# Edge counts and masked attention of a graph network in one written order, with one-hot rows made six chunks ahead

## The chip, the cores and the metric

The kernel runs on one core of a Trainium2 chip. The metric is the device time of one execution in microseconds (us). Three runs of the kernel before gave a median of 616.33 us (615.88 to 616.94).

## The reference

Four layers of a graph network run one after the other on 512 nodes with 512 features. The graph has 16,896 directed edges, sorted by their destination, each of one of two types. The change touches the first layer, an attention over all node pairs that is masked by the edges; cut to its core:

```python
q = (x @ Wq + bq).reshape(N, H, HEAD)          # N = 512, H = 8, HEAD = 64; k and v likewise
scores = jnp.einsum('nhd,mhd->nhm', q, k) / np.sqrt(HEAD)
adj = jnp.zeros((N, N)).at[edge_index[0], edge_index[1]].set(1.0)
scores = jnp.where(adj[:, None, :] == 0, -1e9, scores)
attn = softmax(scores, axis=1)                 # over the heads
attn_out = jnp.einsum('nhm,mhd->nhd', attn, v).reshape(N, D_OUT) @ Wo + bo
h1 = layer_norm(x + attn_out)
return layer_norm(h1 + relu(h1 @ W1 + b1) @ W2 + b2)
```

The softmax runs over the eight heads of one pair of nodes, so that one 128-row tile of pairs needs nothing of another tile. The layers behind it add up neighbours (two layers of a network with batch norm, one graph convolution, two layers with a weight matrix for each edge type). The weight matrices of the last two layers are mixtures of 30 matrices of 512 x 512 each:

```python
w = jnp.einsum('rb,bio->rio', att, basis)      # basis: 30 x 512 x 512, att: 2 x 30
```

This mixture depends on no node, so that it can be worked out at any time before the last layers.

## The kernel before

**Counts.** All layers need the edges as matrices of 512 x 512: how many edges of each type lead from a node to another. The kernel counts them on TensorE. The edges lie in 132 chunks of 128. For each chunk `chunk` (L406) makes two one-hot rows for each edge: `hd`, the destination inside the tile, weighted by the type (VectorE, L416), and `hs`, the source among 512 nodes (ScalarE's Sign, L420, for the chunks of PSUM bank 0; VectorE, L422, for those of bank 1). One matmul (L425) of the two adds the chunk's counts into `cnt`. As the edges are sorted, each of the four destination tiles takes a contiguous span of about 35 chunks; a chunk on a border belongs to two tiles, is made once and is kept. The rows have six buffers a tag. `counted` (L428) decodes a tile's two banks into `Bc` with three copies on ScalarE and three operations on VectorE, and updates the mask `apart`.

**Attention.** It has eight blocks: two halves of 256 nodes (`part`) times four tiles of 128 neighbours (`mt`). `attention` (L477) is a generator of seven steps: two half scores (mask matmuls L484 and key times query L489 into `psc`, which has one buffer, and a copy on ScalarE, L491), the maximum over the heads on VectorE (L494 to L496), the subtraction there and the exp on ScalarE (L498, L499), the sum over the heads as eight matmuls with the identity (by the helper `product`, L244) and a reciprocal on VectorE (L504), the weighting (L506), and the products with v (L514) into `ao`. Blocks 0 to 2 of the first half run beside the counts of tiles 1 to 3, one step for every five chunks; the five other blocks follow two at a time. The products for q and k run beside the counts of tile 0, the four for v beside those of tile 1, one for every eight chunks.

**Basis.** `basis_step` (L181) works off the mixture of basis matrices in 64 steps of four matmuls each (L191), 32 for each of the last two layers. Each takes a 960 KB load on SP's queue, kept four ahead. After each fourth step ScalarE copies the result and stores it to DRAM (`summed`), from where `wrel_load` (L199) fetches it on POOL's queue. The steps are strewn over the program: 4, 6, 6 and 6 in the counts of the four tiles, 10 in the attention, two in the loop with Wo (`basis_step(t % 2)`, L634), four in that with W1 (L658), and the others later.

**Order.** A scheduler sets each engine's order of instructions from their dependencies and its estimate of their times; the order of the program is only where it starts. `tc.keep_in_program_order(...)` holds the instructions that are given to it in the program's order. Before, it holds the basis steps and a few others; the counts and the attention are left to the scheduler. Waits between engines are semaphores, and an engine runs its own instructions in order.

Of the kernel before, what the change touches and what calls it, by code (L numbers as in the profile page):

```python
# [30 lines left out]
LESS = 2.0 ** -12  # L31
MARGIN = 2
SIGNED = (14, 24, 24, 24)
AHEAD = 4
EPS = 1e-5
SLOPE = 0.01
# [30 lines left out]
def gnn_kernel(ctx: ExitStack, tc: tile.TileContext, out: bass.AP, a: dict):  # L67
# [27 lines left out]


    ep = edges.enter_context(tc.tile_pool(name="edges", bufs=1))
    op = edges.enter_context(tc.tile_pool(name="onehot", bufs=6))
    raw = ExitStack()
    rp = raw.enter_context(tc.tile_pool(name="raw", bufs=1))  # L100

# [140 lines left out]
    def product(p, pairs):  # L242
        for i, (lhsT, rhs) in enumerate(pairs):
            nc.tensor.matmul(p, lhsT=lhsT, rhs=rhs, start=(i == 0), stop=(i == len(pairs) - 1))  # L244

    def ts(i):
        return slice(i * P, (i + 1) * P)

    def flip(src, s, dst=None):

        p = ps()
        for k in range(T):
            nc.tensor.transpose(p[:, ts(k)], src[:, s, ts(k)], ident)  # L253
        p = p.rearrange("q (k n) -> q k n", k=T)
        if dst is None:
            return p
        nc.scalar.copy(dst[:, :, ts(s)], p)
# [125 lines left out]
    def project_v():  # L383
        w = weights.take()
        v = made["v"] = big("E")
        bv = rows.take()
        for t in range(T):
            p = ps()
            product(p, [(made["hT"][:, k, ts(t)], w[:, k, :]) for k in range(T)])
            nc.vector.tensor_add(v[:, t, :], p, bv)  # L390
            yield


# [9 lines left out]
    assert all(len(cs) <= 31 for pair in in_bank for cs in pair)  # L403
    kept = {}

    def chunk(c, t, cnt):  # L406

        b = bank_of[c]
        if c in kept:
            hd, hs, first = kept.pop(c)  # L410
        else:
            first = tiles_of[c][0]
            both = len(tiles_of[c]) == 2
            w = P * len(tiles_of[c])
            hd = op.tile([P, 2 * P], F16, name="hd", tag="hd2" if both else "hd", bufs=4 if both else 6)
            nc.vector.tensor_scalar(hd[:, :w], iot[:, P * first:P * first + w], key[:, 0, c:c + 1],  # L416
                                    key[:, 2, c:c + 1], op0=ALU.is_equal, op1=ALU.mult)
            hs = op.tile([P, N], F16, name="hs", tag="hs2" if both else "hs", bufs=4 if both else 6)
            if b == 0:
                nc.scalar.activation(hs, iot, AF.Sign, bias=key[:, 3, c:c + 1])  # L420
            else:
                nc.vector.tensor_scalar(hs, iot, key[:, 1, c:c + 1], None, op0=ALU.is_equal)  # L422
            if both:
                kept[c] = hd, hs, first
        nc.tensor.matmul(cnt[b], lhsT=hd[:, ts(t - first)], rhs=hs,  # L425
                         start=(c == in_bank[t][b][0]), stop=(c == in_bank[t][b][-1]))

    def counted(t, cnt):  # L428

        left = ep.tile([P, N + 1], F32, name="left")  # L430
        nc.scalar.copy(left[:, 1:], cnt[0])
        nc.scalar.activation(left[:, 0:1], cnt[0][:, N - 1:N], AF.Copy, scale=-1.0)
        nc.scalar.copy(Bc[1][:, t, :], cnt[1])
        nc.vector.tensor_sub(Bc[0][:, t, :], cnt[0], left[:, :N])
        for held in (cnt[1], Bc[0][:, t, :]):
            nc.vector.scalar_tensor_tensor(apart[:, t, :], held, 0.0, apart[:, t, :], op0=ALU.is_equal, op1=ALU.mult)

    def typed(t, rest):

# [34 lines left out]
                for i in range(2):  # L474
                    yield 4 * q + 2 * b + i, 2 * q + i, b

    def attention(part, mt):  # L477
        ns = slice(part * NH, (part + 1) * NH)
        qT, kT = made["q"], made["k"]
        sc = pool[0].tile([P, H, NH], F32, name="sc")  # L480
        for q in range(2):
            p = psum[0].tile([P, 2, 2, NH], F32, tag="sc", name="psc", bufs=1)
            for b in range(2):
                nc.tensor.matmul(p[:, b], lhsT=far_off, rhs=apart[:, mt, None, ns].to_broadcast([P, 2, NH]),  # L484
                                 start=True, stop=False)
            for i in range(2):
                for b in range(2):
                    bs = slice(HD * b, HD * b + HD)
                    nc.tensor.matmul(p[:, b, i, :], lhsT=kT[bs, 2 * q + i, ts(mt)], rhs=qT[bs, 2 * q + i, ns],  # L489
                                     start=False, stop=(i == 1))  # L490
            nc.scalar.copy(sc[:, 4 * q:4 * q + 4, :], p.rearrange("p b i n -> p (b i) n"))  # L491
            yield
        half = pool[0].tile([P, H // 2, NH], F32, name="half", bufs=1)
        nc.vector.tensor_max(half, sc[:, 0:4, :], sc[:, 4:8, :])  # L494
        nc.vector.tensor_max(half[:, 0:2, :], half[:, 0:2, :], half[:, 2:4, :])
        nc.vector.tensor_max(half[:, 0, :], half[:, 0, :], half[:, 1, :])  # L496
        yield
        nc.vector.tensor_sub(sc, sc, half[:, 0:1, :].to_broadcast([P, H, NH]))  # L498
        nc.scalar.activation(sc, sc, AF.Exp, scale=HD ** -0.5)  # L499
        yield  # L500
        p = bank("ps")[:, :NH]
        product(p, [(ident, sc[:, j, :]) for j in range(H)])
        rec = pool[0].tile([P, NH], F32, name="rec", bufs=2)
        nc.vector.reciprocal(rec, p)  # L504
        yield
        nc.vector.tensor_mul(sc, sc, rec[:, None, :].to_broadcast([P, H, NH]))  # L506
        yield
        if mt == 0:

            ao[part] = [bank(("ao", "cnt")[part]) for _ in range(2)]  # L510
            for j in range(2):
                nc.tensor.matmul(ao[part][j], lhsT=zero[:, :P], rhs=zero, start=True, stop=False)
        for s, hp, b in heads():
            nc.tensor.matmul(  # L514
                ao[part][hp // 2][HD * b:HD * b + HD, hp % 2 * NH:hp % 2 * NH + NH],
                lhsT=made["v"][:, mt, (2 * hp + b) * HD:(2 * hp + b + 1) * HD], rhs=sc[:, s, :],
                start=False, stop=False)
        if mt == T - 1:
            for j in range(2):
                nc.tensor.matmul(ao[part][j], lhsT=zero[:, :P], rhs=zero, start=False, stop=True)  # L520
                nc.scalar.copy(aoT[:, 2 * j:2 * j + 2, ns], ao[part][j].rearrange("p (i n) -> p i n", i=2))
        yield

    def chain(*gens):
        for g in gens:
# [4 lines left out]
            next(gen, None)  # L530

    proj = chain(project_T(BQ, "C", "q"), project_T(BK, "D", "k"))
    proj_v = project_v()
    for t in range(T):
        cnt = [bank("cnt") for _ in range(2)]
        side = attention(0, t - 1) if t else None
        n = 0
        if t == 1:
            advance(proj_v)
            advance(side)  # L540
        for c in range(*span[t]):
            chunk(c, t, cnt)
            n += 1
            if t == 0 and n == 12:
                select()
                raw.close()
                pool.append(edges.enter_context(tc.tile_pool(name="attn", bufs=3)))
            if t == 0 and n % 4 == 0:
                advance(proj)
            if t == 1 and n % 8 == 0:  # L550
                advance(proj_v)
            if t and n % 5 == 3:
                advance(side)
            if n % 6 == 5 and (t or n > 16):
                basis_step()
        if t:
            for _ in side:
                pass
        counted(t, cnt)
        if t == 0:  # L560
            for _ in proj:
                pass
        if t == 1:
            for _ in proj_v:
                pass
            aoT = big("B")

    under = []
    for block in ((0, 3), (1, 0), (1, 1), (1, 2), (1, 3), None, None):
        if len(under) == 2 or not block:  # L570
            for _ in under.pop(0):
                pass
            basis_step(1)
        if under:
            advance(under[-1], 2)
        if block:
            under.append(attention(*block))
            advance(under[-1], 2)
            basis_step(1)
    edges.close()  # L580
    psum.append(ctx.enter_context(tc.tile_pool(name="psum2", bufs=1, space=bass.MemoryType.PSUM)))
    turn[0] = ["pr", "pr", "pg"]
# [42 lines left out]
    for t in range(T):  # L625
        p = ps()
        product(p, [(aoT[:, k, ts(t)], w[:, k, :]) for k in range(T)])
        v = h1[:, t, :]
        nc.vector.tensor_add(v, p, bo)
        nc.vector.tensor_add(v, v, h[:, t, :])  # L630
        norm_affine(v, g1, be1)
        if t:
            flip(h1, t - 1, h1T)
            basis_step(t % 2)  # L634
    rest = [late.tile([P, T, N], F32, tag="wrel", name="rest", bufs=2) for _ in range(2)]
    for t in range(T):
        typed(t, rest)
# [10 lines left out]
    for half in range(2):  # L648
        ns = slice(half * NH, (half + 1) * NH)
        for i in range(2):  # L650
            for m in range(T):
# [3 lines left out]
                nc.scalar.activation(ff[i][:, m, ns], p[:, :NH], AF.Relu, bias=cols[:, at:at + 1])  # L655
                if half == 0 and i == 0 and m == 2:
                    flip(h1, T - 1, h1T)
            basis_step(1)  # L658
    w = [weights.take(), weights.take()]
    b2, g2, be2 = (rows.take() for _ in range(3))  # L660
    y, hT = big("A"), big("D")
# [289 lines left out]
```

## Time and profile before

| what | value |
|---|---|
| median of three runs | 616.33 us (615.88 to 616.94) |
| the profiled execution | 616.2 us |
| its span | 614.4 us |
| mean granted TensorE clock | 0.967 |
| TensorE (PE) busy | 554.8 us, 90% of the span, 2226 instructions |
| TensorE weight loads (PEld) | 277.1 us, 45% |
| VectorE (DVE) | 275.4 us, 45%, 590 instructions |
| ScalarE (ACT) | 199.1 us, 32%, 319 instructions |
| GpSimd (POOL) | 32.9 us, 5%, 70 instructions |
| DMA | 94.06 MB, 153 GB/s over the span |

The profiled execution is one, and its span starts and ends with the first and last instruction; its time includes 1.8 us around that. A row of a timeline has the start in us from the span's beginning, the duration in us, the engine, the line and the operation, output and inputs with partitions x elements and type, how many instructions it joins, and in brackets how long the engine idled before it and whose result ended that idle time. Three of the costliest groups, with the busy time, the mean ns of one and the idle time before them:

```profile
L420 ACT ACTIVATE hs<-iot,key 128x512 f16<-128x512 f16 x80 | 52.9, 713 | 17.0 <-PE cnt L425 16.4
L425 PE MATMUL cnt<-hs,hd 128*128 128x512 f16 x144 | 41.3, 391 | 6.3 <-DVE hs L422 5.6
L491 ACT COPY sc<-psc 128x1024 f32<-128x1024 f32 x16 | 16.1, 1006 | 27.9 <-PE psc L489 27.9
```

### The profile page before, as it was taken

The page shows a single profiled execution, that of the slowest core. Times are in us where ns is not written, and L with a number is a line of the kernel's source. Part 1 is how long each engine was busy: PE and PEld are TensorE (multiplying, and loading weights), DVE is VectorE, ACT ScalarE, POOL GpSimd, SP SyncE. Part 2 cuts the span into 40 slices and gives each one's busy share as a digit, 9 for nine tenths or more (in the row PEclk, how much of TensorE's full clock was granted, in tenths as well). Part 3 has the DMA queues.
Part 4 walks back from the last instruction along what each step waited for, and adds up shares of the span by engine and source line. Part 5 has one row for each costly group of instructions (what it writes and reads, how often), then busy time and mean ns, then how long its engine had stood idle before and what let it go on. Part 6 is the DMA issues. An engine that isn't in the chain of part 4 may idle for free.

```text
span 614.4 us, 5939 instructions
## 1 busy us (share of the span) xinstructions
PE 554.8 (90%) x2226; PEld 277.1 (45%) x2226; DVE 275.4 (45%) x590; ACT 199.1 (32%) x319; POOL 32.9 (5%) x70
## 2 busy tenths in 40 slices
PE   2999999797878867899999999999869899999997
PEld 1433343333344433367544453353324556545653
DVE  4732665665464852489076632422511841103110
ACT  3534566465333410222233221522332260104100
POOL 4000000000000000010202100000000200000000
PEclk9999999797998988899999999999969999999999
DMA  8998779899783672468987856786699000003000
GB/s 290 217 243 177 202 173 253 190 203 199 165 191 79 146 178 64 97 179 198 313 199 200 217 152 156 177 206 197 180 225 221 8 18 2 0 1 138 1 34 34
DMA packets 42345, 94.06 MB, mean 153 GB/s; under 512 B 1949, under 2 KB 2345, under 8 KB 41801
## 3 DMA queue, kind: packets, MB, share of 16 engines
q1 hardware_dynamic: 34296, 67.32, 48.3%
q0 software_dynamic: 5136, 21.07, 10.6%
q10 hardware_dynamic: 2880, 5.24, 2.6%
q8 instruction: 21, 0.34, 0.2%
q14 instruction: 12, 0.09, 0.1%
HBM read 88.38 MB, written 5.24 MB: 152 GB/s over the span
## 4 chain that ended last, share of the span: by engine, by line
PE 49%; issue 35%; DMA 7%; DVE 3%; ACT 1%; POOL 1%; POOLq 0%; ACTq 0%
PE pr L244 11%; PE acc L868 9%; PE pg L244 8%; DMA row<-in_rows 5%; PE acc L833 5%; PE ao L244 4%; PE bas L191 4%; PE ps L244 3%; DMA basis<-in_basis 2%; PE cnt L425 2%; PE acc L704 1%; PE acc L244 1%; PE pr L253 1%; POOL w L138 0%; ACT hs L420 0%
## 5 line engine op out<-in xcount | busy, mean ns | idle before, releaser
L191 PE MATMUL bas<-basis,wide 120*32 120x512 f32 x512 | 72.7, 629 | 7.0 <-DMA basis<-in_basis 6.9
L420 ACT ACTIVATE hs<-iot,key 128x512 f16<-128x512 f16 x80 | 52.9, 713 | 17.0 <-PE cnt L425 16.4
L416 DVE TENSOR_SCALAR hd<-iot,key 128x128 f16<-128x128 f16 (+1 forms) x132 | 36.5, 314 | 35.6 <-PE cnt L425 35.4
L244 PE MATMUL ps<-sc,ident 128*128 128x256 f32 x128 | 37.8, 451 | 14.0 <-ACT sc L499 13.6
L425 PE MATMUL cnt<-hs,hd 128*128 128x512 f16 x144 | 41.3, 391 | 6.3 <-DVE hs L422 5.6
L244 PEld LDWEIGHTS ps<-sc,ident 128*128 128x128 f32 x128 | 28.0, 227 | 25.3 <-ACT sc L499 16.6
L425 PEld LDWEIGHTS <-hd 128*128 128x128 f16 x144 | 12.6, 99 | 43.7 <-issue 19.1
L244 PE MATMUL pr<-w,bigB 128*128 128x512 f32 x64 | 30.3, 620 | 0.0
L868 PE MATMUL acc<-wrel,bigC 128*128 128x512 f32 x64 | 29.7, 593 | 0.0
L191 PEld LDWEIGHTS bas<-basis,wide 120*32 120x32 f32 x512 | 10.8, 110 | 35.0 <-issue 25.0
L491 ACT COPY sc<-psc 128x1024 f32<-128x1024 f32 x16 | 16.1, 1006 | 27.9 <-PE psc L489 27.9
L504 DVE RECIPROCAL rec<-ps 128x256 f32<-128x256 f32 x8 | 14.0, 1755 | 23.0 <-PE ps L244 23.0
L269 ACT ACTIVATE sd<-mv,eps 128x1 f32<-128x1 f32 x32 | 9.2, 293 | 44.8 <-DVE mv L267 43.7
L499 ACT ACTIVATE sc<-sc 128x2048 f32<-128x2048 f32 x8 | 15.3, 1910 | 21.1 <-DVE sc L498 21.1
L494 DVE TENSOR_TENSOR half<-sc 128x1024 f32<-128x1024 f32 x8 | 9.8, 1225 | 27.5 <-ACT sc L491 27.5
L244 PE MATMUL pr<-bigE,w 128*128 128x512 f32 x48 | 21.2, 592 | 0.0
L244 PE MATMUL pr<-bigD,w 128*128 128x256 f32 x88 | 20.3, 381 | 0.0
L244 PEld LDWEIGHTS pr<-w,bigB 128*128 128x128 f32 x64 | 12.6, 203 | 17.1 <-issue 15.9
L489 PE MATMUL psc<-bigC,bigD 64*128 64x256 f32 x128 | 19.5, 404 | 0.0
L244 PE MATMUL ao<-bigB,w 128*128 128x512 f32 x40 | 19.1, 616 | 0.0
L506 DVE TENSOR_TENSOR sc<-sc,rec 128x2048 f32<-128x2048 f32 x8 | 18.3, 2287 | 0.2
L422 DVE TENSOR_SCALAR hs<-iot,key 128x512 f16<-128x512 f16 x52 | 18.0, 349 | 0.6 <-DVEq L360 0.6
(293 smaller groups left out, 894.3 us busy)
## 6 DMA issues: line engine op xcount, KB each, us to landing
basis<-in_basis SPq DMA_DIRECT2D x64, 960.0 KB, 9.3
w<-in_W POOLq DMA_DIRECT2D x4, 1024.0 KB, 5.9
summed<-sums ACTq DMA_DIRECT2D x16, 256.0 KB, 8.1
wrel<-summed POOLq DMA_DIRECT2D x4, 1024.0 KB, 5.7
row<-in_rows POOLq DMA_DIRECT2D x12, 256.0 KB, 7.8
w<-in_conv_W1T POOLq DMA_DIRECT2D x2, 1024.0 KB, 7.1
w<-in_conv_W2T POOLq DMA_DIRECT2D x2, 1024.0 KB, 6.6
w<-in_root POOLq DMA_DIRECT2D x2, 1024.0 KB, 6.5
```

Source lines behind the costliest of these rows:

```text
L191: tc.keep_in_program_order(nc.tensor.matmul(sums[0][32 * j:32 * j + 32, :], lhsT=wide[l][:KB, 24 - 8 * g:56 - 8 * g], rhs=t[:, j, :], star ...
L244: nc.tensor.matmul(p, lhsT=lhsT, rhs=rhs, start=(i == 0), stop=(i == len(pairs) - 1))
L416: nc.vector.tensor_scalar(hd[:, :w], iot[:, P * first:P * first + w], key[:, 0, c:c + 1], key[:, 2, c:c + 1], op0=ALU.is_equal, op1=ALU.mult)
L420: nc.scalar.activation(hs, iot, AF.Sign, bias=key[:, 3, c:c + 1])
L422: nc.vector.tensor_scalar(hs, iot, key[:, 1, c:c + 1], None, op0=ALU.is_equal)
L425: nc.tensor.matmul(cnt[b], lhsT=hd[:, ts(t - first)], rhs=hs, start=(c == in_bank[t][b][0]), stop=(c == in_bank[t][b][-1]))
L489: nc.tensor.matmul(p[:, b, i, :], lhsT=kT[bs, 2 * q + i, ts(mt)], rhs=qT[bs, 2 * q + i, ns], start=False, stop=(i == 1))
L491: nc.scalar.copy(sc[:, 4 * q:4 * q + 4, :], p.rearrange("p b i n -> p (b i) n"))
L499: nc.scalar.activation(sc, sc, AF.Exp, scale=HD ** -0.5)
L506: nc.vector.tensor_mul(sc, sc, rec[:, None, :].to_broadcast([P, H, NH]))
L833: nc.tensor.matmul(self.out[t], lhsT=self.hT[:, k, ts(t)], rhs=self.root[:, k, :], start=(k == 0), stop=False)
L868: nc.tensor.matmul(self.out[t], lhsT=self.uT[r][:, k, ts(t)], rhs=wrel[r][:, k, :], start=False, stop=(r == 1 and k == T - 1))
```

## The change

The counts of tiles 1 to 3 and all of the attention stand in one written order on TensorE, VectorE and ScalarE: the helper `on` puts each of their instructions under `keep_in_program_order`. Tile 0 with q and k stays with the scheduler.

`chunk` is split in two, `rows_of` and `count`. In tiles 1 to 3 the rows of a chunk are emitted six chunks (`BEHIND`) ahead of their matmul, and the pool has seven buffers for them in place of six. The steps of the attention, now methods of a class `Block` with the same instructions, stand at set places of a tile's count: `weigh` of the block before behind count 1, `shift` behind count 8, `values` of the block before behind count 15, `sums` behind count 22, basis steps behind counts 5, 18 and 30. At the tile's end come `counted`, two basis steps and the scores of the next block. Of the four products for v the first stands before tile 1, two in it (behind counts 2 and 12) and one in tile 2 (behind count 12). The blocks of the second part follow in a loop: values of block j-2, scores of j+1, shift of j, a basis step, weigh of j-1, sums of j.

The basis steps move: 26 instead of 32 stand before the stage with Wo (3 in tile 0, 15 with tiles 1 to 3, 8 in the attention), 3 instead of 2 in the loop with Wo, 6 instead of 4 in that with W1; the other places ask for as many as before, and three steps more are left for the last place in the program, which works off what remains.

```diff
-    op = edges.enter_context(tc.tile_pool(name="onehot", bufs=6))
+    op = edges.enter_context(tc.tile_pool(name="onehot", bufs=BEHIND + 1))
...
+    def on(ins):
+        return tc.keep_in_program_order(ins)
...
-    for t in range(T):
-        cnt = [bank("cnt") for _ in range(2)]
-        side = attention(0, t - 1) if t else None
...
+    ahead = [(t, c) for t in range(1, T) for c in range(*span[t])]
+    for _, c in ahead[:BEHIND]:
+        rows_of(c)
+    for n, (t, c) in enumerate(ahead):
+        at = c - span[t][0]
+        if at == 0:
+            cnt = [bank("cnt") for _ in range(2)]
+        count(c, t, cnt)
+        if n + BEHIND < len(ahead):
+            rows_of(ahead[n + BEHIND][1])
+        if t > 1 and at == 1:
+            blocks[t - 2].weigh()
+        if at == 8:
+            blocks[t - 1].shift()
+        if t == 1 and at in (2, 12):
+            advance(proj_v)
+        if t == 2 and at == 12:
+            advance(proj_v)
+        if t > 1 and at == 15:
+            blocks[t - 2].values()
+        if at == 22:
+            blocks[t - 1].sums()
+        if at in (5, 18, 30):
+            basis_step()
+        if c == span[t][1] - 1:
+            counted(t, cnt)
+            basis_step(2)
+            blocks[t].scores()
...
-            under.append(attention(*block))
-            advance(under[-1], 2)
-            basis_step(1)
+    for j in range(3, 8):
+        if j > 3:
+            blocks[j - 2].values()
+        if j + 1 < len(blocks):
+            blocks[j + 1].scores()
+        else:
+            basis_step(1)
+        blocks[j].shift()
+        basis_step(1)
+        blocks[j - 1].weigh()
+        blocks[j].sums()
+    blocks[7].weigh()
+    blocks[6].values()
+    basis_step(2)
+    blocks[7].values()
...
-            basis_step(t % 2)
+            basis_step(1)
...
-            basis_step(1)
+            basis_step(1 + i)
```

## The prediction

> **What bounds the kernel now.** I read the cores' view (one core, 614.4 us, clock 0.967), then the page's busy slices, then a table of windows cut at the borders of the stages that the diff touches, then the TensorE timeline inside them. The windows (start:end, length, then busy us of PE, PEld, DVE, ACT, POOL with instructions, granted clock, DMA share, GB/s):
>
> ```profile
> 18.00:64.00 46.00, 46.00 (x151) 18.78 (x151) 19.31 (x74) 17.94 (x29) 2.38 (x6) 1.00 0.93 220
> 64.00:99.00 35.00, 34.73 (x164) 14.49 (x161) 22.78 (x57) 21.59 (x32) 1.29 (x2) 1.00 0.78 200
> 99.00:133.00 34.00, 29.32 (x144) 12.06 (x143) 20.50 (x54) 19.73 (x30) 0.00 (x0) 0.90 0.90 197
> 133.00:164.50 31.50, 27.11 (x132) 11.52 (x125) 17.86 (x41) 16.79 (x25) 0.00 (x0) 0.89 0.82 184
> 164.50:247.00 82.50, 62.34 (x347) 33.92 (x345) 43.71 (x32) 22.55 (x21) 0.00 (x0) 0.92 0.60 134
> ```
>
> TensorE is the bound nearly everywhere. Count tile 0 has no hole, tile 1 0.3 us, tiles 2 and 3 4.7 and 4.4 us, and the attention alone (164.5 to 247) 20.2 us. So a better order has 29.5 us of holes to win, and the clock lost behind them. The holes in the PE timeline (start, length, group, then idle time and who ended it):
>
> ```profile
> 112.79 0.38 PE L425 MATMUL cnt<-hs,hd 128*128 128x512 f16 x1 [2.29 <-DVE hs L422]
> 114.25 2.08 PE L244 MATMUL ps<-sc,ident 128*128 128x256 f32 x4 [1.08 <-ACT sc L499]
> 148.71 6.45 PE L244 MATMUL ps<-sc,ident 128*128 128x256 f32 x16 [0.99 <-ACT sc L499]
> 168.39 0.59 PE L484 MATMUL psc<-apart,far_off 128*128 128x512 bf16 x2 [1.11 <-ACT sc L491]
> 256.21 0.73 PE L253 MATMUL pr<-ident,bigC 128*128 128x128 f32 x4 [2.17 <-DVE bigC L284]
> 256.88 1.93 PE L191 MATMUL bas<-basis,wide 120*32 120x512 f32 x8
> ```
>
> See that TensorE waits for VectorE rows while VectorE shifts scores, then for the exp, and that sums of 3.45 us (80.68 to 84.13) cost 6.45 us behind such a hole. That exp chain, in the DVE and ACT timelines:
>
> ```profile
> 178.81 1.22 DVE L494 TENSOR_TENSOR half<-sc 128x1024 f32<-128x1024 f32 x1 [2.94 <-ACT sc L491]
> 180.07 0.69 DVE L495 TENSOR_TENSOR half<-half 128x512 f32<-128x512 f32 x1
> 180.80 0.43 DVE L496 TENSOR_TENSOR half<-half 128x256 f32<-128x256 f32 x1
> 181.26 2.29 DVE L498 TENSOR_TENSOR sc<-sc,half 128x2048 f32<-128x2048 f32 x1
> 183.58 1.91 ACT L499 ACTIVATE sc<-sc 128x2048 f32<-128x2048 f32 x1 [4.32 <-DVE sc L498]
> ```
>
> Shift is 4.74 us, exp 1.91; `weigh` (L504, L506) is 4.05.
>
> **Part 1, counts with attention blocks 0 to 2** (end of tile 0's counts at 58.4 to the last count at 163.4: 105.0 us). TensorE's work in the new order, by start-to-start times of the PE timeline: 109 count matmuls at 0.23 (six from 94.60 to 96.00) 25.1; four v products at 3.44, 13.8; six half scores at 1.59 (101.08 to 102.67) 9.5; three sums at 3.45, 10.4; two `values` at 1.93 and their opening 0.5, 4.4; basis steps at 1.00: 14 instead of 19, 14.0. Together 77.2. The same sum for before (19 basis steps, three `values`) is 84.1, plus 9.4 of holes and 5.6 of slow clock (two sums): 99.1 of 105.0; the missing 5.9 is switching between short runs, and I carry it over.
>
> New waits. (a) The second half of each scores waits for ACT's copy with nothing between: 1.1 (168.39), three times 3.3. (b) scores(1), scores(2) wait for `counted`: copy 0.59, 0.18, three DVE operations of 0.69, 0.2 of handover, less two basis steps: 1.0 each, 2.0; before, the counts of the next tile lay there. (c) `shift` follows count 8, with rows up to chunk 14 out. PE then has six counts (1.4) and, in tiles 1 and 2, a v product (3.4). Chunk 15's row stands behind shift on VectorE and, when ScalarE makes it, behind exp too: 4.74+1.91+0.71=7.4. Hole 2.6 in tiles 1 and 2; in tile 3 VectorE makes it (4.74+0.31+0.35=5.4) and no v covers: 4.0. Together 9.2. `weigh` stands where scores' copies and a basis step cover it: 0. (d) Clock: a hole of this kind cost 2.8 (6.45 against 3.45, less tails) before; between 0 and 8.4 for three, half: 4.2. Sum 77.2+5.9+3.3+2.0+9.2+4.2=101.8: **3.2 us less**, though five basis steps and one `values` (6.9) left the stretch. Six rows ahead do not span a 4.7 us shift.
>
> **Part 2, the attention alone** (163.4 to the first product with Wo at 246.9: 83.5). ScalarE's order is now copies of j+1, then exp of j. Per block on TensorE: `values` 1.93, scores 1.59+1.1+1.59, then copy 1.0, exp 1.91 and handover (3.0; a basis step lies inside), sums 3.45: 12.7. Start: two basis steps, 1.0 for `counted`, scores(3) with its waits 5.4, 8.4; j=3 without `values` 10.8; j=4 to 6 38.0 and 1.0 for opening and closing; j=7 without scores 7.4; the tail (`values` 6 and 7, two basis steps, closing, copy to aoT) 8.0. Sum 73.6. VectorE needs only 8.8 per block.
>
> Four holes of 2.0 remain here. The Trainium skill (TensorE: Matmul & The Clock Gate, "HAM oscillation — how this bites in real kernels") says that only idle gaps beyond about 3.4 us throttle; by it they cost nothing, 73.6. The trace has a 2.17 us hole before 256.21 and then a basis step at 1.93 for 1.06 and transposes at 0.73 for 0.60, and the product after that 4.35 for 3.60: 1.7 lost. By the row 73.6+6.8=80.4. A hole of 1.75 (203.44) cost nothing, and 2.0 lies between: half, 77.0. **6.5 us less.**
>
> **Part 3, the moved basis steps.** 26 instead of 32 stand before the Wo stage; three go into the Wo and W1 stages, three to the end beside the last layer. TensorE is full there (8.00 of 8.00, 7.00 of 7.00 in windows 262 to 284; 60 of 60 in 500 to 560): 3.0+3.0 **more**. But steps 31 and 32 now end behind the first half of W1, and the gather of relation weights on POOL's queue needs them; the POOL timeline has it (L203), then R's cast and the next load:
>
> ```profile
> 290.07 0.53 POOL L203 DMA_DIRECT2D wrel<-summed  x1 [18.10 <-DVE Bc L450]
> 296.91 0.61 POOL L593 CAST R<-Bc 128x512 fp32r<-128x512 f32 x1 [6.30 <-DMA row<-in_rows]
> 297.46 0.76 POOL L138 DMA_DIRECT2D w<-in_W  x1
> ```
>
> and, in the ACT timeline, the copy that VectorE's `u` releases:
>
> ```profile
> 291.38 0.63 ACT L456 ACTIVATE z<-u 128x512 f32<-128x512 f32 x1 [2.17 <-DVE u L454]
> ```
>
> Before, typed() ended that wait 23.3 us into W1 (266.8). After: first half with its steps 17.4, copy 0.6, store 8.1 (median of the issues' table), handover: 26.4. Behind the gather on POOL stand the strays branch, R's casts, and W2's second half; behind the branch, by the new order, VectorE's `u` (L462), ScalarE's `z` (L464), then relu copies that free W1's banks. PE runs out of banks about 2.0 us earlier. W2's second half was issued 7.3 us before its use and takes 5.8; it now comes about 1 later than needed, with DMA at 0.99 and three more 960 KB loads in that stretch. Together 0 to 9, I take 5.0, and 1.0 of clock. The bunched steps near 450 already wait 5.5 and 1.4 for DMA and remain; their loads shift: 0 to 4, 1.0. Sum **13.0 more**. Later inputs of layer 2 land in idle DMA time and cost nothing. v beside the counts is the same four products, beside tiles 1 and 2.
>
> **Sum**: 616.2-3.2-6.5+13.0=**619.5** (span 614.4 and 1.8 around it, unchanged); the runs' median is 616.33, the same within what matters.
>
> **Rivals.** *The order works and the clock holds* (faster): no hole throttles, and switches shrink by 3: part 1 becomes 94.6 (-10.4), part 2 73.6 (-9.9), part 3 +9.0: 604.9. It decides if holes up to 3.4 us keep full clock. For it: the page; fewer changes of kind of work. Against: 2.17 us above. *Every hole throttles and the gate bites*: +4.2, +3.4, +4 in part 3: 631. For it: three shift holes and four exp holes per run, two engines stalled in series. Against: 1.75 without loss. *It does nothing net*: the scheduler before had nearly this overlap, and gains equal moved steps: 616.3. For it: DVE's order before already ran rows between shift's parts; against: PE's holes move by whole us.
>
> **Chances.** Forecast 0.38 (617.5 to 625), works 0.30, throttled 0.22, nothing 0.10. Measurement tells 0.2% (1.2 us) from no change. Faster 0.30 (0.27 of the second, 0.03 of the last), same 0.10 (0.03 and 0.07 of these two), slower 0.60. Range 606 to 630.
>
> **What would show it.** Right: holes of 2.5 to 4 us after six counts in each tile, ended by a row from ScalarE or VectorE; 12.7 us between blocks with 2.0 ended by exp; the gather on POOL later relative to W1 than 23.3, and waits of W1 products for banks and of the second W2 product for w. Wrong: clock 1.00 from 64 to 247 (then 605), or the W1 and W2 stages without holes.

## The result, and where the time went

The changed kernel takes 624.18 us (median of 18 executions, 616.33 to 631.01) against 617.04 (612.5 to 619.02): ratio 1.0065, interval 1.0036 to 1.0094. A second set gave a median of 626.2 (616.77 to 630.13) and a ratio of 1.0192 (1.015 to 1.0234). The ratios leave out executions that lie more than 1.5% above the kernel's fastest, and for this kernel those are many, so that medians say more (7.1 us slower). The first profiled execution is a long one (629.0 us, span 627.2). What follows reads a later one of 616.8 us (span 615.0), almost as long as the profile of before, so that gains and losses can be set side by side; it is near the short end of the kernel's executions, and the long one is set beside it where they differ.

The table of windows of the changed kernel, cut where the prediction cut that of before (columns as there):

```profile
20.00:57.50 37.50, 37.50 (x113) 15.47 (x111) 12.07 (x52) 11.94 (x19) 1.07 (x2) 1.00 0.81 196
57.50:90.00 32.50, 28.32 (x124) 12.68 (x123) 19.05 (x53) 19.55 (x30) 0.52 (x1) 1.00 0.56 139
90.00:123.00 33.00, 28.34 (x147) 12.49 (x139) 22.29 (x56) 19.74 (x31) 1.30 (x2) 0.95 0.82 197
123.00:154.50 31.50, 25.72 (x141) 10.96 (x141) 20.35 (x50) 20.64 (x32) 0.00 (x0) 0.95 0.73 165
154.50:228.80 74.30, 57.54 (x363) 33.03 (x363) 49.18 (x35) 23.68 (x25) 0.00 (x0) 1.00 0.59 135
```

TensorE now has more holes beside the counts (4.2, 4.7 and 5.8 us), and still the stretch is shorter. Its holes in the TensorE timeline:

```profile
80.79 0.38 PE L432 MATMUL cnt<-hs,hd 128*128 128x512 f16 x1 [2.33 <-ACT hs L423]
...
140.72 0.38 PE L432 MATMUL cnt<-hs,hd 128*128 128x512 f16 x1 [3.31 <-DVE hs L425]
...
160.10 0.59 PE L497 MATMUL psc<-apart,far_off 128*128 128x512 bf16 x2 [1.11 <-ACT sc L505]
...
170.22 3.72 PE L520 MATMUL ps<-sc,ident 128*128 128x256 f32 x16 [1.93 <-ACT sc L515]
...
281.62 3.56 PE L245 MATMUL pr<-bigD,w 128*128 128x256 f32 x8 [4.24 <-ACT bigE L696]
```

The first two are the waits for a row behind `shift`, the third the copy between two half scores, the fourth the exp. The last is new and lies in the W1 stage.

In the attention alone (both windows hold ten basis steps) the new order has 16.8 us of holes for 20.2, and a TensorE busy time of 57.5 us for 62.3, at a granted clock of 1.00 for 0.92: more than half of the gain there is the clock. What went were two long waits near the end of the old order, for the exp and for the weighting of the last blocks; its TensorE timeline has them:

```profile
229.01 1.22 PE L244 MATMUL ps<-sc,ident 128*128 128x256 f32 x2 [6.01 <-ACT sc L499]
230.16 3.24 PE L514 MATMUL cnt<-sc,bigE 128*64 128x256 f32 x16
...
241.87 2.70 PE L514 MATMUL cnt<-sc,bigE 128*64 128x256 f32 x16 [4.25 <-DVE sc L506]
```

The `values` behind the first takes 3.24 us, where 2.00 is usual, at a granted clock of 0.60. All stages, from TensorE's timelines (start of the first instruction of a kind to the next such start):

| stage | before | changed | difference |
|---|---|---|---|
| last step of tile 0 to the last count | 105.0 | 96.9 | -8.1 |
| attention alone, to the first product with Wo | 83.5 | 74.4 | -9.1 |
| Wo and W1, to the first product with W2 | 54.3 | 61.6 | +7.3 |
| first turn of W2 | 7.5 | 8.0 | +0.5 |
| rest of W2, second layer, graph convolution, to its W product | 147.7 | 149.4 | +1.7 |
| to the first transpose of the relation layers | 29.3 | 30.9 | +1.6 |
| to the first product with their weights | 28.2 | 32.8 | +4.7 |
| to the end | 100.6 | 103.5 | +2.9 |

The new order wins 17.2 us, and 18.7 are given back behind it. (The start of this execution was 0.8 shorter.) The long execution, cut in the same way, wins 15.7 and gives back about 30.5. Of the 12.2 us between the two spans 9.6 lie in one row of the table, the first turn of W2: 17.6 us for 8.0. The median execution is between them.

**Why W1 and W2 wait.** POOL's timeline around the gather of the relation weights (L204):

```profile
278.57 0.53 POOL L204 DMA_DIRECT2D wrel<-summed  x1 [25.18 <-DMA summed<-sums]
287.16 1.17 POOL L634 CAST R<-Bc 128x512 fp32r<-128x512 f32 x2 [8.06 <-DMA row<-in_rows]
288.28 0.76 POOL L139 DMA_DIRECT2D w<-in_W  x1
```

and VectorE's and ScalarE's:

```profile
279.15 1.29 DVE L462 TENSOR_TENSOR u<-Bc,Bc 128x512 f32<-128x512 f32 x2 [7.83 <-POOLq L681]
```

```profile
279.88 0.63 ACT L464 ACTIVATE z<-u 128x512 f32<-128x512 f32 x1 [8.36 <-DVE u L462]
...
281.12 0.45 ACT L696 ACTIVATE bigE<-pr,cols 128x256 f32<-128x256 f32 x1
```

The gather waits for the store of basis step 32, which now falls behind W1's first half. The branch for strays (L681) stands behind it on POOL; VectorE's `u` waits until POOL gets to the branch, ScalarE's `z` waits for `u`, the relu copies stand behind `z`, and TensorE has no PSUM bank until one of them is done: 4.24 us. Then POOL idles 8.06 us more. The profile names a row's load, which had long landed (the last one was issued at 252.77). The branch itself waits, as the view of its line L681 has it (count, then ns of the shortest, the median and the longest, then the first and last start):

```profile
L681 POOLq EVENT_SEMAPHORE  x5: 17/43/7118, 279.1 to 279.4; - x5
L681 POOLq INC_SWDGE_SEM  x1: 472/472/472, 286.6 to 286.6; - x1
```

One of its semaphore instructions lasts 7.1 us, and the next instruction starts at 286.6, when the gather of 278.57 lands (8.0 us from issue to landing). Nothing from inside the branch is in the trace. So the second half of W2 is asked for only when the gather has landed, at 288.28, though the buffer of W1's first half was free at 274.4. TensorE wanted it at 294.1 and waited 0.25 us. In the other profiles with this late gather it waited 3.73 (e4), 5.79 (e2) and, in the long execution, 7.05 us:

```profile
302.22 6.48 PE L245 MATMUL pr<-w,bigB 128*128 128x512 f32 x8 [7.05 <-DMA w<-in_W]
```

In all four the load was asked for only 1.0 to 2.1 us ahead of W2's first product; what differs more is how long it took to land: 6.0, 8.6, 10.6 and 11.8 us. Why it differs so much isn't shown. The product behind the wait takes 6.48 us in place of 3.70.

**Why the last layers start slowly.** Windows from the first transpose of the relation layers to the first product with their weights, of before:

```profile
485.70:513.80 28.10, 27.74 (x120) 17.62 (x121) 12.52 (x25) 13.31 (x22) 0.98 (x2) 1.00 0.03 10
```

and of the changed kernel:

```profile
478.70:511.50 32.80, 32.67 (x120) 20.68 (x121) 12.29 (x24) 12.76 (x21) 0.00 (x0) 0.84 0.14 34
```

The same 120 instructions take 4.7 us longer at a clock of 0.84. Ahead of them stands a hole of 3.23 us (before: 1.32 and 0.36). ScalarE's timelines, first of before, then of the changed kernel:

```profile
483.00 0.29 ACT L269 ACTIVATE sd<-mv,eps 128x1 f32<-128x1 f32 x1 [8.63 <-DVE mv L267]
```

```profile
475.52 0.59 ACT L197 COPY sums<-bas 128x512 f32<-128x512 f32 x1 [10.05 <-PE bas L192]
476.13 0.33 ACTq L198 DMA_DIRECT2D summed<-sums  x1
476.51 0.29 ACT L274 ACTIVATE sd<-mv,eps 128x1 f32<-128x1 f32 x1 [0.40 <-ACT sums L197]
```

Every fourth basis step ends with a ScalarE copy and a store. Three steps are out of place by then, so that the fourth one now falls here: the copy stands ahead of the square root of the normalization and waits for TensorE's step.

### The profile page after: what moved, and what is told of

It reads as the page before. It is cut to its first block, busy times and chain, and to the rows that moved or that the text cites. A ratio compares the mean times of both kernels' runs of the same rounds, so it can differ in the third digit from the quotient of the medians.

```text
span 627.2 us, 5942 instructions
## 1 busy us (share of the span) xinstructions
PE 553.3 (88%) x2226; PEld 279.8 (45%) x2226; DVE 276.1 (44%) x590; ACT 197.9 (32%) x319; POOL 32.1 (5%) x70
## 4 chain that ended last, share of the span: by engine, by line
PE 46%; issue 38%; DMA 11%; DVE 2%; ACT 1%; POOL 1%; POOLq 0%; ACTq 0%; another core or an unknown queue 0%
PE pr L245 14%; PE pg L245 11%; PE acc L909 9%; DMA row<-in_rows 5%; PE acc L874 5%; PE bas L192 4%; DMA basis<-in_basis 2%; DMA w<-in_W 2%; DMA x<-in_x 1%; PE pr L258 1%; PE acc L745 1%; PE acc L245 1%; POOL w L139 0%; POOL row L156 0%; DVE st L270 0%
## 5 line engine op out<-in xcount | busy, mean ns | idle before, releaser
L192 PE MATMUL bas<-basis,wide 120*32 120x512 f32 x512 | 68.1, 620 | 10.1 <-DMA basis<-in_basis 8.9
L423 ACT ACTIVATE hs<-iot,key 128x512 f16<-128x512 f16 x80 | 51.3, 710 | 10.8 <-PE cnt L432 10.4
L432 PE MATMUL cnt<-hs,hd 128*128 128x512 f16 x144 | 40.0, 393 | 9.2 <-ACT hs L423 5.6
L245 PE MATMUL pr<-w,bigB 128*128 128x512 f32 x64 | 34.3, 689 | 8.2 <-DMA w<-in_W 7.1
L520 PE MATMUL ps<-sc,ident 128*128 128x256 f32 x128 | 31.1, 398 | 7.7 <-ACT sc L515 7.7
L520 PEld LDWEIGHTS ps<-sc,ident 128*128 128x128 f32 x128 | 25.1, 199 | 15.9 <-ACT sc L515 11.3
L197 ACT COPY sums<-bas 128x512 f32<-128x512 f32 x16 | 9.3, 583 | 40.9 <-PE bas L192 40.5
L497 PE MATMUL psc<-apart,far_off 128*128 128x512 bf16 x32 | 9.5, 378 | 12.0 <-ACT sc L505 10.0
L245 PEld LDWEIGHTS pr<-bigD,w 128*128 128x128 f32 x88 | 16.5, 191 | 7.3 <-ACT bigE L696 4.4
L514 DVE TENSOR_TENSOR sc<-sc,half 128x2048 f32<-128x2048 f32 x8 | 18.3, 2292 | 0.5
```

The source lines that it names most:

```text
L192: tc.keep_in_program_order(nc.tensor.matmul(sums[0][32 * j:32 * j + 32, :], lhsT=wide[l][:KB, 24 - 8 * g:56 - 8 * g], rhs=t[:, j, :], star ...
L423: keep(nc.scalar.activation(hs, iot, AF.Sign, bias=key[:, 3, c:c + 1]))
L432: keep(nc.tensor.matmul(cnt[b], lhsT=hd[:, ts(t - tiles_of[c][0])], rhs=hs, start=(c == in_bank[t][b][0]), stop=(c == in_bank[t][b][-1])))
L514: on(nc.vector.tensor_sub(sc, sc, half[:, 0:1, :].to_broadcast([P, H, NH])))
L520: on(nc.tensor.matmul(self.total, lhsT=ident, rhs=self.sc[:, j, :], start=(j == 0), stop=(j == H - 1)))
```

## The experiments

Theory A: the new order wins, and the basis steps that were moved late lose it again, by the gather on POOL and by the copy of each fourth step. Theory B, the rival: whoever arrives earlier waits longer for the same loads, or TensorE is simply full.

| kernel | median us (runs) | range | ratio to before |
|---|---|---|---|
| before (four sets) | 616.5 to 617.6 (7 to 28) | 612.5 to 620.4 | 1 |
| e1_fill: six steps back, in holes | 598.51 (6) | 597.0 to 600.4 | 0.969 (0.9658 to 0.9722) |
| e2_realign: last three steps back in W2 | 617.21 (22) | 608.8 to 623.9 | 0.9946 (0.9921 to 0.9971) |
| e3_gather: three steps from W1 to holes | 612.28 (7) | 608.3 to 613.9 | 0.9907 (0.9871 to 0.9942) |
| e4_steps_only: before, steps moved | 644.9 (6) | 643.1 to 649.0 | 1.0445 (1.0406 to 1.0485) |
| e8_hold: gather behind the branch | 616.44 (14) | 615.2 to 620.7 | 1.0011 (0.9988 to 1.0034) |
| e5_spread: e1, shift in four parts | 590.07 (6) | 590.0 to 593.5 | 0.9586 (0.9549 to 0.9623) |
| e6_gaps: e1, steps between half scores | 606.28 (6) | 604.6 to 607.6 | 0.9829 (0.9792 to 0.9866) |
| e7_both: e5 and e6 | 596.9 (6) | 593.6 to 600.1 | 0.9692 (0.9654 to 0.9731) |
| e9_v: e1, v ahead of the counts | 610.86 (5) | 607.6 to 611.7 | 0.9896 (0.9857 to 0.9935) |
| e10_eight: e1, rows eight ahead | 594.99 (4) | 593.0 to 597.2 | 0.9648 (0.9607 to 0.969) |

### after_again: the changed kernel once more

> The changed kernel again, for a second execution of it beside the others on one chip: the attention ends 17 to 18 us earlier than before; if the losses behind it are as in the first profile, waits of about 3 us for banks in W1, 5 to 7 for W2's second half and 3.2 ahead of the last layers come back; the time 1.003 to 1.010 of before.

Its profile is the one read above: 18.1 us earlier at the first product with Wo, banks 4.24, the last layers 3.23; the wait for W2's second half was 0.25 only, outside what was expected, and the ratio of 1.0192 is above it too.

### e1_fill: the six steps back ahead of Wo

```diff
-        if at in (5, 18, 30):
+        if at in (5, 18, 30) or (t > 1 and at == 14):
...
-        basis_step(1)
+        basis_step(2 if j < 7 else 1)
...
-            basis_step(1)
+            basis_step(t % 2)
...
-            basis_step(1 + i)
+            basis_step(1)
```

> The changed kernel with the six basis steps put back ahead of the Wo stage, in TensorE's holes: one more step behind each exp in blocks 3 to 6, one behind count 14 in tiles 2 and 3; the Wo and W1 loops as before the change. Theory A (the steps that were moved late make the loss: the gather on POOL and behind it W2's second half come late, and each fourth step's ScalarE copy falls in a bad place): the attention keeps all but about 1.5 us of its 17.7, and every later stage takes what it took before the change, so 14 to 17 us less than before, about 601. Theory B (the loss behind W1 is the price of arriving early: the same loads of W2 and basis matrices over the same DMA are simply waited for later): no more than 5 us less than before, 611 or more.

598.51, 18.4 less than before: theory A, and somewhat more than it said. In its profile counts and attention take 174.2 us, 3.0 more than in the changed kernel, for six steps of 1.0; the first two W2 products, in TensorE's timeline, follow without a wait:

```profile
171.63 3.72 PE L520 MATMUL ps<-sc,ident 128*128 128x256 f32 x16 [1.07 <-ACT sc L515]
...
282.88 3.70 PE L245 MATMUL pr<-w,bigE 128*128 128x512 f32 x8
286.42 3.60 PE L245 MATMUL pr<-w,bigB 128*128 128x512 f32 x8
```

A step in the exp's hole shortens it from 1.93 to 1.07. The new order itself is worth 18 us (598.5 against 616.9) once as many steps stand ahead of Wo as before.

### e4_steps_only: the moved steps without the new order

```diff
-            if n % 6 == 5 and (t or n > 16):
+            if n % (7 if t else 6) == 5 and (t or n > 17):
...
-            basis_step(1)
+            basis_step(1 if block else 0)
...
-            basis_step(t % 2)
+            basis_step(1)
...
-            basis_step(1)
+            basis_step(1 + i)
```

> The kernel before with only the basis steps as in the changed kernel (3 in tile 0, 15 with tiles 1 to 3, 8 in the attention, 3 and 6 in the Wo and W1 loops), order left to the scheduler. Theory A: the attention wins at most the 6 us of the six steps, the gather is late and W1 and W2 lose 8 to 15 us, the end 3 to 8: 5 to 15 us slower than before, that is, the moved steps alone are slower than the whole change. Theory B (the fixed order with its early end makes the later waits): within 3 us of before.

644.9, 28.0 more than before: theory A's sign, and twice its size. Its windows for counts and attention, and its TensorE timeline in W1 and W2:

```profile
58.40:163.40 105.00, 94.19 (x416) 39.93 (x414) 62.04 (x151) 57.68 (x83) 1.29 (x2) 0.92 0.74 173
163.40:248.90 85.50, 63.53 (x336) 34.34 (x332) 44.05 (x32) 23.24 (x24) 0.00 (x0) 0.88 0.48 110
```

```profile
302.33 2.64 PE L244 MATMUL pr<-bigD,w 128*128 128x256 f32 x8 [3.13 <-ACT bigE L655]
...
318.67 6.34 PE L244 MATMUL pr<-w,bigB 128*128 128x512 f32 x8 [3.73 <-DMA w<-in_W]
```

Counts and attention end at 248.9, no earlier than before (246.9), though six steps are gone; from the last step of tile 0 they take 3.9 us more (192.4). In the old order the steps had cost nothing there, and without them the granted clock is lower (0.88 in the attention alone, 0.92 before); that the steps' absence lowers it isn't shown. Theory A had counted on 6 us less in this stretch, hence most of its miss. The two waits of the changed kernel come back without its order. So, by the medians, the order wins 18 to 21 (e1 against before, the changed kernel against e4), and the moved steps cost 26 to 28; the change is their sum.

### e3_gather and e8_hold: only the gather

e3 takes three steps from the W1 loop to the exp's holes, so that step 32 ends with the Wo stage:

```diff
-        basis_step(1)
+        basis_step(2 if j < 6 else 1)
...
-            basis_step(1 + i)
+            basis_step(min(1, half + i))
```

> The changed kernel with three basis steps taken from the W1 loop into the holes behind the exps of blocks 3 to 5, so that step 32 ends with the Wo stage and the gather can start before W1's first half is done; from W1's end on the steps stand as in the changed kernel. Theory A: no 3.1 us wait for banks in W1, W2's second half in time (wait 0 instead of 7.1), three steps hidden: 10 to 15 us less than the changed kernel, 5 to 9 less than before. Theory B (W2's second half waits for DMA however early it is asked for): at most 4 us less than the changed kernel.

612.28, and 1.6% less than the changed kernel by the ratios (0.9907 against 1.0065), 11.9 by the medians: theory A, at its lower edge (4.6 to 5.7 less than before, where 5 to 9 was expected). No wait for banks is left, W2's second half is asked for at 279.06 and waited for 0.64 us, and the 3.23 us hole ahead of the last layers is still there.

e8 leaves every step where the change put it and alters POOL's order alone, by putting the casts of `R1` and the gathers in the program's order:

```diff
-            nc.gpsimd.tensor_copy(r[:, t, :], counts[:, t, :])
+            (on if tag == 'R1' else lambda ins: ins)(nc.gpsimd.tensor_copy(r[:, t, :], counts[:, t, :]))
...
-            nc.gpsimd.dma_start(t, of[:, T * r:T * r + T, :])
+            on(nc.gpsimd.dma_start(t, of[:, T * r:T * r + T, :]))
```

> The changed kernel with its basis steps where they are; only POOL's order is another: the two gathers of the first relation layer's weights stand behind the branch, the loads of W2 and the later layers' weights, in place of ahead of the branch. TensorE, VectorE, ScalarE and SP keep their order. Theory A (the gather ahead of the branch is what makes the late steps dear: the branch waits for the gather's landing, VectorE's u, ScalarE's copies and W2's second half wait for the branch): the waits of 3.1 for banks and of 7.1 for W2's second half are gone with the steps still late, 8 to 13 us less than the changed kernel, about as the kernel with three steps moved forward (9.7 less). Theory B (the steps' own time on a full TensorE and their loads are the loss): within 3 us of the changed kernel.

By the medians 7.7 less than the changed kernel, by the ratios 3.3: between the theories by one count and short of A by the other. The profile settles it. POOL's timeline, and TensorE's later:

```profile
252.09 0.62 POOL L156 DMA_DIRECT2D row<-in_rows  x1 [0.31 <-DVE bigC L289]
274.08 0.76 POOL L139 DMA_DIRECT2D w<-in_W  x1 [21.36 <-PE pg L245]
...
420.89 0.75 POOL L139 DMA_DIRECT2D w<-in_root  x1 [15.81 <-PE pg L245]
421.63 1.09 POOL L204 DMA_DIRECT2D wrel<-summed  x2
```

```profile
437.18 1.94 PE L192 MATMUL bas<-basis,wide 120*32 120x512 f32 x8 [11.08 <-DMA basis<-in_basis]
```

No semaphore instruction of the branch lasts over 0.04 us now. W2's second half is asked for 14 us earlier, both waits are gone, and W2's first step starts at 291.16 in place of 298.44 (before: 308.69). Five of these 7.3 us are lost again where the two gathers, 1 MB each, were put: beside a burst of basis steps, which wait 11.08 and 2.41 us for their loads in place of 5.95 and 2.35. The scatter is gone too, 615.2 to 620.7 in 14 runs against 616.3 to 631.0. In e2, which keeps the late gather, it is 15 us as well; in e1 and e3, with an early gather, 3 and 6. The two profiled executions of the changed kernel differ mainly in the turn of W2 that waits for this load (9.6 of 12.2 us). So the waiting time for W2's second half very likely makes the scatter, but e4 with a late gather scatters by only 6.

### e2_realign: only the end

```diff
-        basis_step(1)
+        basis_step(2 if t < 3 else 1)
```

(in the loop of W2)

> The changed kernel with the last three basis steps taken from the program's last place into the loop of W2 (two a turn in three of four turns), so that from W2's end on the steps stand where they stood before the change, while the gather stays late. Theory A: the waits for banks and for W2's second half remain (W2's first basis step no earlier than before the change), three steps cost 3.0 in W2, and the end wins 2.7 of steps and the 3 to 7 us of the hole before the last layers and its slow clock: 2 to 7 us less than the changed kernel. Theory B (the end's slow stretch is chance of the profiled run): within 1 us of the changed kernel.

617.21, 1.2% less than the changed kernel by the ratios and 7.0 by the medians: theory A, at its upper end. Its TensorE timeline where the changed kernel has the hole of 3.23 and the slow clock:

```profile
482.99 0.66 PE L258 MATMUL pr<-ident,bigD 128*128 128x128 f32 x4 [1.32 <-ACT bigD L284]
484.00 0.66 PE L258 MATMUL pr<-ident,bigD 128*128 128x128 f32 x4 [0.36 <-ACT bigD L284]
484.50 1.03 PE L245 MATMUL pg<-cols,bigE 128*128 128x2 f32 x8
485.39 1.10 PE L874 MATMUL acc<-w,bigE 128*128 128x512 f32 x2
```

These are the holes of before. In the changed kernel the two rows of the last kind took 2.05 (1.10 here). W1 and W2 still wait 2.86 and 5.79, as expected.

### e10_eight, e9_v and e5_spread: the wait behind the shift

e10 is e1 with `BEHIND = 8`; e9 takes all four v products ahead of tile 1's counts; e5 cuts the shift in four:

```diff
-        if at == 8:
-            blocks[t - 1].shift()
+        if at in (5, 9, 12, 16):
+            blocks[t - 1].shift((5, 9, 12, 16).index(at))
...
-        if at == 22:
+        if at == 25:
```

> The kernel with six steps in the holes (598.5) with rows eight chunks ahead of their counts in place of six (nine buffers a tag). If rows fill the time of the shift, each wait at count 15 is shorter by two counts of 0.23: 1.4 us less in sum; nothing if VectorE is so busy that it isn't eight rows ahead when the shift starts.

3.5 less by the medians: as expected in kind, and more than the 1.4 expected. Its wait behind the shift is 1.69 in tile 1 where e1 has 2.33, none in tile 2, and 2.69 in tile 3 where e1 has 2.95.

> The kernel with six steps in the holes (598.5) and all four products for v ahead of tile 1's counts. If the place of v is worth nothing (same products, TensorE full on both sides): within 1.5 us of it. If v is the cover for the shift in tiles 1 and 2: their waits at count 15 grow from 2.3 and 1.4 by up to 3.4 each, 3 to 7 us more.

12.3 more, beyond both. Its waits at count 15 are 4.74 and 4.43 where e1 has 2.33 and 1.40, and the basis step behind the first takes 1.94 in place of 1.06; counts and attention take 181.7 us against 174.2. So v is the cover for the shift: its place beside the counts is part of the gain. The profiled execution, the shortest of the five, is 9.0 longer than e1's: 7.5 of it there and 1.6 in the Wo stage, by a slow product (5.27 us for 3.70) behind a hole of 2.17 that e1 has too. The rest of the 12.3 stands in executions without a profile.

> The kernel with six steps in the holes (598.5), and in the counts the shift cut in four parts (behind counts 5, 9, 12 and 16, subtraction and exp in halves, rows between them) and the sums behind count 25. If the row six chunks ahead behind one shift of 4.7 us is what stops TensorE at count 15, its waits of 2.3, 2.3 and 2.9 for rows go, and the attention ends 3 to 6 us earlier (two of them have a basis step in them already); if VectorE's work in sum is the limit, the wait only moves and nothing is won.

8.4 less than e1. In the counts the longest wait for a row is 1.77; the halved subtraction and exp also let each exp start under the subtraction, so that the exp's hole in blocks 4 to 6 is 0.21 in place of 1.07, which I had not counted. This version is the fastest of all: 590.07, 4.1% less than before.

### e6_gaps and e7_both: a step too many

```diff
-            blocks[j + 1].scores()
+            blocks[j + 1].scores(1)
```

(one basis step behind the copy of the first half)

> The kernel with six steps in the holes (598.5), and one basis step more between the two halves of the scores of blocks 4 to 7, where TensorE waits 1.11 us for ScalarE's copy. The four steps go from the program's end, so that every fourth step still falls in the same place. If a step is free in a hole of its own length and costs 1.0 where TensorE is full, 2 to 4 us less than that kernel; if the loads (960 KB each) can't follow, waits for the basis appear in the attention and nothing is won.

A miss: 7.8 more than e1. The timelines of ScalarE and of TensorE in block 5:

```profile
195.88 1.91 ACT L517 ACTIVATE sc<-sc 128x2048 f32<-128x2048 f32 x1
197.69 0.58 ACT L197 COPY sums<-bas 128x512 f32<-128x512 f32 x1
```

```profile
198.32 1.06 PE L192 MATMUL bas<-basis,wide 120*32 120x512 f32 x8 [2.40 <-ACT sums L197]
```

The step behind the second half is now the fourth of its four; its copy stands behind the exp on ScalarE, and the next step waits for the one bank of the basis. DMA is busy for 0.97 of the stretch from 145 to 229 (0.78 in e1). The steps also ran out ahead of the last layers: a hole of 3.43 us is there, without any copy in it (1.32 in e1), and the stage behind it takes 31.8 us for 28.2.

> Both of the two last edits together: if they are independent, the sum of their gains, 5 to 9 us less than the kernel with six steps in the holes, about 591; the clock full through counts and attention.

596.9, only 1.6 less than e1: a miss, as e6 was no gain. The measured parts do add up: e5's 8.4 less and e6's 7.8 more give 597.9.

## Why the prediction was right, and where it wasn't

The direction and the range held (619.5 in 606 to 630, measured 624.2), and the mechanism that was to decide it, the late gather on POOL's queue, is one of the two that the experiments show. That the point came out close is luck: two errors of opposite sign met. -9.7 was predicted ahead of the Wo stage and +13.0 behind it; the profile shows -17.2 and +18.7, and that of the long execution -15.7 and about +30.5.

**Part 1, -3.2, measured -8.1.** The work and the waits were right: the waits add up to 14.5 us, as summed. What failed is the step "the missing 5.9 is switching between short runs, and I carry it over", with 4.2 for the clock: together 10.1, of which 5.2 are there. Two slow rows of `values` (3.66 and 3.34 us in place of 2.00) make 3.0 of these, so that the clock was near and only 2.2 are left of the 5.9. An unexplained rest of the old order was taken for a cost of the work. By its own terms this was the rival in which the order works (94.6; measured 96.9).

**Part 2, -6.5, measured -9.1.** Terms and holes were right (12.9 us from one block's sums to the next for 12.7, 1.93 of it ended by exp). Half of the clock loss that the 2.17 us hole suggested, 3.4 us, was booked for four holes of 2.0. In the profile read here they cost nothing at a granted clock of 1.00, as the rule of the Trainium skill ("TensorE: Matmul & The Clock Gate", "HAM oscillation — how this bites in real kernels") had it. But holes below its bound of 3.4 us aren't always free; the section names longer gaps as those to avoid, and the "only" was the prediction's. In the long execution the third of the same four holes is followed by sums of 5.35 us in place of 3.72 (granted clock 0.67):

```profile
195.28 5.35 PE L520 MATMUL ps<-sc,ident 128*128 128x256 f32 x16 [1.93 <-ACT sc L515]
```

And beside the counts the holes of 2.39 and 3.31 are followed by the two slow `values`, at 0.52 and 0.57. The window of the first, in the profile read here:

```profile
110.71:114.30 3.59, 3.59 (x18) 1.90 (x17) 0.25 (x1) 1.66 (x3) 0.00 (x0) 0.52 1.00 321
```

Neither the row nor the rule gives a price for one hole.

**Part 3, +13.0, measured +18.7.** The three steps in the Wo and W1 stages, the wait for banks and the late load of W2's second half came as described. Bank wait 4.24 for 2.0; the load was late by 0.25 us here and by 7.05 in the long execution, for "about 1", since it took 6.0 to 11.8 us to land and not 5.8. So these stages, with 9.0 in the sum (3.0 of steps, 5.0, 1.0 of clock), gave back 7.8 here and 18.1 there. "Their loads shift: 0 to 4, 1.0" is near (+1.7 in the table's row). The last steps' own 3.0 are there too (+2.9). What failed is the sum's treatment of the last three steps as three steps: it left out that every fourth one carries a copy on ScalarE. That copy costs 6.3 us ahead of the last layers (1.6 of hole, 4.7 of clock), and no term stood for it. Also, "26 instead of 32" was booked as a gain of 6.9 for five steps and one `values`; in the old order taking the steps out won nothing, as e4 shows, and in the new one six of them cost 3.0 (e1).

"v beside the counts is the same four products" was wrong as a price of nothing: e9 shows that they are the cover for the shift.

## What to carry to other kernels

Before filler work is moved, ask what hangs at its end: here a copy with every fourth step, a store, a gather in a queue, and a branch behind that gather. Put it where the engine has holes and its buffers and loads are ready, and keep its phase to what follows. And an order written out by hand can win all that it should, and lose it again some stages behind; read the stages behind it too.

## What the runs showed of the hardware

The branch, from whose inside nothing ran, still held POOL until the gather ahead of it had landed: one of its semaphore instructions lasts 7.1 us here, 5.2 in e1 with an early gather, 5.4 before, and none over 0.04 us in e8 with the gather behind it. The profile put the wait down to another load.

In all 13 profiles of this case a hole of 2.17 us stands ahead of the same transposes of the Wo stage. In seven (the kernel before among them) the product behind it was slow, 4.35 to 5.27 us in place of 3.70 (4.94 at a granted clock of 0.73 in the long execution of the changed kernel); in the six others, the short execution of the same kernel among them, it ran at full speed. So the same hole cost about 1.7 us or nothing.

The stage from the first transpose of the relation layers to the first product with their weights took 28.2 us in the six profiles with a hole of 1.32 us ahead of it, and 31.8 to 33.1 in the seven with one of 3.23 to 3.55.
